# Elementwise chains kept in place in PSUM in a four-layer image network on one core

## The chip, the cores and the metric

The kernel runs on one core of a Trainium2 chip. The core has five engines that each work through their own queue of instructions in order and wait for each other by semaphores: TensorE (PE, matrix products into PSUM), VectorE (DVE), ScalarE (ACT), GpSimd (POOL) and SyncE (SP, which here only issues DMA transfers). SBUF is the large on-chip memory; PSUM is the small one that the matrix products write, in eight banks of 512 float32 columns by 128 partitions. The metric is the device time of one execution in microseconds; three runs of the kernel before gave 12745.85, 12742.49 and 12727.7, median 12742.49.

## The reference

Input and output are 8 images of 64 channels of 64x64, float32. Four layers follow each other.

- Layer 0: attention over the 4096 pixels with softmax(x^T x / 8) and values relu(bn(w1 x)), then a 3x3 depthwise convolution, batch norm and relu, a 1x1 convolution with batch norm, and the residual: `return out + x`.
- Layer 1: two blocks of window attention, 8x8 windows, 8 heads of 8 channels, each with an MLP. The second block shifts the image by four pixels, and windows at the wrap get a mask of -100 on the scores: `attn = softmax(q k^T + bias + mask)`.
- Layer 2: nine taps, each the shifted image times a factor by pixel and one by channel, summed; then a leaky relu, `a = where(out >= 0, out, 0.1 * out)`, a 1x9 convolution and a residual.
- Layer 3: a state-space scan in four directions with 128 channels and 16 states, h = h * exp(dt * A) + dt * B * u, y = sum(C * h); then `y = ln(y) * silu(z)`, a projection and a residual; then `gelu(aggr(...)) * x` added to the result, where aggr mixes four depthwise convolutions of different resolution.

## The kernel before, in words

Images go in pairs, p = 0 to 3, two images of 64 channels filling the 128 partitions. For each pair a generator `front(p)` does layers 0 to 2 and the inputs of the scan (`layer0`, `layer1`, `layer2`, `scan_sources`), `scans(p)` does the recurrence, and `back(p)` does what follows the scan. `scans` runs its own steps and, between them, pulls pieces of the generators beside it: `front(p+1)` and `back(p-1)`. So the front of pair 0 runs without scans, the scans of pairs 0, 1 and 2 run beside a front (and, from pair 1 on, a back), and the scans of pair 3 have only `back(2)` and, in their last steps, `back(3)` beside them. The numbers that the generators yield are costs; `scans` pulls until the sum of yields keeps pace with its steps. From the order so written a scheduler makes the order in each engine's queue when the program is built.

A scan step handles two of the 16 states over 512 pixels: POOL forms B * du for both (`products`, L1754, 128x1024), ACT forms exp(dt * A) into a PSUM bank (L1776), DVE runs the recurrence (L1779), POOL or DVE multiplies with C (L1790, L1793), and PE sums over the states (L1805). B and C rows come by DMA from rows that each unit wrote before (`fetch`, L1746, and `inputs`, L1729).

PSUM is given out by `bank`: three banks with the tag "f" serve front and back, three with the tag "da" the scans, one "acc" (through `total`) and one "y". While `turn` is not negative, in the first front and when only `back(3)` is left, `bank` alternates between "f" and "da".

The places that the change touches, all on tiles of 128x512 or 128x256 float32:

- `layer0`, last part: per chunk of 512 pixels nine DVE taps, ACT's relu (L1342), a matmul into the bank `pw` (L1344), ACT's batch norm from `pw` into the SBUF tile `t` (L1346), DVE's addition X + t (L1348).
- `window_row`, `scores`: two banks of scores from PE (L1431); DVE adds the bias and writes SBUF (L1444); where a window lies at the wrap DVE adds the mask in SBUF (L1448, 30 instructions per pair, all in the second block); ACT takes the exponential (L1449); PE multiplies with the values (L1459).
- `layer2`: PE sums nine taps into `acc` (L1576); ACT copies `acc` to the tile `t1` (L1580); DVE takes max(0.1 * acc, t1) into the padded tile `a` (L1581), which nine matmuls read (L1584). There are two tiles `a`, for even and odd chunks.
- `back`, first part: per chunk and image a matmul into the bank `pc` (L1235), the square on ACT (L1237), its mean by PE into `pv` (L1239), two ACT instructions to the inverse deviation `sd` (L1241, L1242); DVE forms u = pc * g * sd in SBUF (L1845) and u = (u + b) * z (L1846), and PE projects u (L1847) into `po`, which DVE adds to X (L1849).
- `back`, last part: nine DVE taps into `sacc` (L1251), a copy to SBUF by ACT (L1886), four matmuls into the bank `pa` (L1888, L1892), GELU by ACT from `pa` into the SBUF tile `ge` (L1900), DVE's product ge * F (L1901) and DVE's addition X + ge (L1902), and the store of the output.

Of the kernel before, what the change touches and what calls it, by code (L numbers as in the profile page):

```python
# [9 lines left out]
F32 = mybir.dt.float32  # L10
AF = mybir.ActivationFunctionType
ALU = mybir.AluOpType
# [5 lines left out]
P = 128  # L18
CH = 512
# [1140 lines left out]
class _Direct:  # L1160
# [104 lines left out]
    def layer0(self, p):  # L1265


        nc, tc, w, net, half = self.nc, self.tc, self.w, self.net, self.HALF
        X = self.flat("X")
        nc.sync.dma_start(X, self.net.x[2 * p : 2 * p + 2].rearrange("b c h w -> (b c) (h w)"))  # L1270
        att = self.padded("att")
        VT = self.flat("VT").rearrange("p (t c) -> p t c", c=P)

        def at(rows, t):
            return X[rows, t * P : (t + 1) * P]

        with self.work("w0") as wk:
            for g in range(8):
                pv = self.bank("pval", (P, 4, P))
                nc.tensor.matmul(pv, lhsT=net.ones[0:1, :], rhs=net.b1row.rearrange("o a c -> o (a c)").unsqueeze(1).to_broadcast([1, 4, P]), start=True, stop=False)  # L1280
                for j in range(4):
                    nc.tensor.matmul(pv[:, j, :], lhsT=at(slice(0, P), 4 * g + j), rhs=net.w1bd, start=False, stop=(j == 3))
                nc.scalar.activation(VT[:, 4 * g : 4 * g + 4, :], pv, AF.Relu)
                yield 3

            parts = wk.tile([P, 2, 32, NCH], F32, name="parts", tag="parts", bufs=1)
            self.dense = 1
            for jc in range(NCH):
                po = self.total("po")

                def weigh(t, es):
                    for im in range(2):
                        nc.tensor.matmul(  # L1293
                            po[half[im]], lhsT=VT[:, t, half[im]], rhs=es[im], start=(t == 0), stop=(t == 31)
                        )

                last = None
                for t in range(32):
                    ss = [self.bank(f"s{im}") for im in range(2)]
                    for im in range(2):  # L1300
                        nc.tensor.matmul(  # L1301
                            ss[im], lhsT=at(half[im], t), rhs=X[half[im], jc * CH : (jc + 1) * CH], start=True, stop=True
                        )
                    es = []
                    for im in range(2):
                        e = wk.tile([P, CH], F32, name="e", tag="e", bufs=6)
                        nc.scalar.activation(  # L1307
                            e, ss[im], AF.Exp, scale=C**-0.5, accum_out=parts[:, im, t, jc : jc + 1]
                        )
                        es.append(e)  # L1310
                    if last is not None:
                        weigh(*last)
                    last = (t, es)
                    yield 3.6
                weigh(*last)
                nc.vector.tensor_copy(self.rows(att, jc), self.img(po))  # L1316

            self.dense = 0
            sums = net.sums[:, p]
            nc.vector.tensor_reduce(sums, parts, AX.X, ALU.add)  # L1320
            rec = wk.tile([P, 2, 32], F32, name="rec", tag="rec", bufs=1)
            nc.vector.reciprocal(rec, sums)
            for g in range(8):
                pr = self.bank("prec")
                for j in range(4):
                    for im in range(2):
                        nc.tensor.matmul(
                            pr[half[im], j * P : (j + 1) * P],
                            lhsT=rec[:, im, 4 * g + j : 4 * g + j + 1].to_broadcast([P, 64]),
                            rhs=w["ident"],  # L1330
                            start=True,
                            stop=True,
                        )
                d = self.rows(att, g)
                nc.vector.tensor_tensor(d, d, self.img(pr), ALU.mult)
                yield 3
        with self.work("w0b") as wk:
            for c in range(NCH):
                acc = self.bank("cacc", (P, 8, 64))
                yield from self.dwconv(acc, att, 8 * c, 8, w["dw2"], None, 0.52)  # L1340
                cv = wk.tile([P, 8, 64], F32, name="cv", tag="cv")
                nc.scalar.activation(cv, acc, AF.Relu, scale=net.bn23[:, 0:1], bias=net.bn23[:, 1:2])  # L1342
                pw = self.bank("pw")
                nc.tensor.matmul(pw, lhsT=w["w3bd"], rhs=cv, start=True, stop=True)  # L1344
                t = wk.tile([P, CH], F32, name="t", tag="t")
                nc.scalar.activation(t, pw, AF.Identity, scale=net.bn23[:, 2:3], bias=net.bn23[:, 3:4])  # L1346
                x = X[:, c * CH : (c + 1) * CH]
                nc.vector.tensor_tensor(x, x, t, ALU.add)  # L1348
                yield 2.25
        return X  # L1350

# [64 lines left out]
    def window_row(self, i, wy, X, now, ahead, wk):  # L1416
# [6 lines left out]
        def scores(x):  # L1423

            es = []
            ss = [self.bank(f"w_s{g}", (P, 2, 4, 64)) for g in range(2)]
            for j in range(2):
                for g in range(2):
                    for im in range(2):
                        rows = slice(64 * im + 32 * g, 64 * im + 32 * g + 32)  # L1430
                        nc.tensor.matmul(  # L1431
                            ss[g][half[im], j],
                            lhsT=K[rows, 64 * (x + j) : 64 * (x + j) + 64],
                            rhs=qx[rows, x + j],
                            start=True,
                            stop=True,
                        )
            kinds = [2 * (wy == 7) + (x + j == 7) if shift else 0 for j in range(2)]
            for g in range(2):
                hs = slice(4 * g, 4 * g + 4)  # L1440
                e = self.share(self.wide, 4 + self.nth % 4).rearrange("p (j h q) -> p j h q", j=2, h=4)
                self.nth += 1
                b = bias[:, 0, hs].unsqueeze(1).to_broadcast([P, 2, 4, 64])
                nc.vector.tensor_tensor(e, ss[g], b, ALU.add)  # L1444
                for j in range(2):
                    if kinds[j]:
                        m = net.smask[:, kinds[j] : kinds[j] + 1].to_broadcast([P, 4, 64])
                        nc.vector.tensor_tensor(e[:, j], e[:, j], m, ALU.add)  # L1448
                nc.scalar.activation(e, e, AF.Exp)  # L1449
                es.append(e)  # L1450
            return es
# [83 lines left out]
    def layer2(self, X):  # L1535
# [11 lines left out]
        with tc.tile_pool(name="w2", bufs=2) as wk:  # L1547
            net.load(wk, (5,))
            cf = net.channel_filters(X, wk, self.pf, "f")
            for c in range(NCH):  # L1550
# [25 lines left out]
                    nc.tensor.matmul(acc, lhsT=w["ident"], rhs=tap, start=(t == 0), stop=(t == TAPS - 1))  # L1576
                    yield 2.7
                a = acts[c % 2]
                t1 = wk.tile([P, 8, 64], F32, name="t1", tag="t1", bufs=1)
                nc.scalar.activation(t1, acc, AF.Copy)  # L1580
                nc.vector.scalar_tensor_tensor(a[:, :, 4:68], acc, 0.1, t1, ALU.mult, ALU.max)  # L1581
                py = self.total("py", (P, 8, 64))
                for t in range(TAPS):
                    nc.tensor.matmul(  # L1584
# [242 lines left out]
    def back(self, p):  # L1827
# [5 lines left out]
        with tc.tile_pool(name="w4", bufs=2) as wk:  # L1833
            for c in reversed(range(NCH)):
# [3 lines left out]
                for im in range(2):  # L1838
                    y = self.share(big, im)
                    z = self.share(big, 2 + im)  # L1840
                    nc.sync.dma_start(y, self.kept["y", 2 * p + im][:, cols])
                    nc.sync.dma_start(z, self.kept[2 * p + im][2][:, cols])
                    pc, sd = self.normed(wk, lambda pc: [(pc, y)], w["cen128"], w["avg128"], net.eps[:, 0:1])
                    u = wk.tile([P, CH], F32, name="u", tag="u")
                    nc.vector.scalar_tensor_tensor(u, pc, w["on_g"], sd, ALU.mult, ALU.mult)  # L1845
                    nc.vector.scalar_tensor_tensor(u, u, w["on_b"], z, ALU.add, ALU.mult)  # L1846
                    nc.tensor.matmul(po[half[im]], lhsT=w["opT"], rhs=u, start=True, stop=True)  # L1847
                    yield 4.2
                nc.vector.scalar_tensor_tensor(X[:, cols], po, w["outproj_b"], X[:, cols], ALU.add, ALU.add)  # L1849
# [5 lines left out]
        with tc.tile_pool(name="w5", bufs=1) as wk:  # L1855
# [25 lines left out]
            for c in range(NCH):  # L1881
# [7 lines left out]
                for i in range(1, 4):  # L1889
# [6 lines left out]
                        start=False,  # L1896
                        stop=(i == 3),
                    )
                ge = wk.tile([P, 8, 64], F32, name="ge", tag="ge", bufs=2)
                last = nc.scalar.activation(ge, pa, AF.Gelu, bias=w["aggr_b"])  # L1900
                nc.vector.tensor_tensor(ge, ge, self.rows(F, c), ALU.mult)  # L1901
                nc.vector.tensor_tensor(X[:, cols], X[:, cols], ge.rearrange("p a b -> p (a b)"), ALU.add)  # L1902
                nc.sync.dma_start(out[:, cols], X[:, cols])
                yield 3.5
            net.log_exp(last)
# [51 lines left out]
```

## Time and profile before

| what | value |
|---|---|
| median of the runs (lowest, highest) | 12742.49 us (12727.7, 12745.85) |
| the profiled execution | 12767.64 us |
| its span, first to last instruction | 12765.8 us |
| mean granted clock of TensorE | 0.819 |
| front of pair 0, no scans | about 0 to 1830 us |
| layer 0's residual in the fronts of pairs 1, 2, 3 (L1348) | 2832 to 2957, 5876 to 5998, 8832 to 8955 us |
| shifted window attention of pairs 1, 2, 3 (L1444) | 3420 to 3745, 6451 to 6764, 9411 to 9721 us |
| back's first part of pairs 0, 1, 2, 3 (L1845) | 4514 to 4797, 7473 to 7763, 10431 to 10988, 12413 to 12662 us |
| back's last part of pairs 0, 1, 2, 3 (L1901) | 4849 to 4965, 7823 to 7938, 11209 to 11542, 12708 to 12757 us |

The profile gives for each engine its busy time, and for groups of equal instructions the busy time, the mean duration and the idle time of the engine just before them with what ended it. An engine's busy time includes time in which an instruction has started and is held up inside the engine; a wait for a semaphore, before it starts, counts as idle. So a group whose instructions do equal work and differ in duration tells of a hold-up inside. The stages of the table run one after the other, and each has an engine of its own that is fullest; the share of an engine over the whole span says little of any of them.

### The profile page before, as it was taken

The page shows a single profiled execution, that of the slowest core. Times are in us where ns is not written, and L with a number is a line of the kernel's source. Part 1 is how long each engine was busy: PE and PEld are TensorE (multiplying, and loading weights), DVE is VectorE, ACT ScalarE, POOL GpSimd, SP SyncE. Part 2 cuts the span into 40 slices and gives each one's busy share as a digit, 9 for nine tenths or more (in the row PEclk, how much of TensorE's full clock was granted, in tenths as well). Part 3 has the DMA queues.
Part 4 walks back from the last instruction along what each step waited for, and adds up shares of the span by engine and source line. Part 5 has one row for each costly group of instructions (what it writes and reads, how often), then busy time and mean ns, then how long its engine had stood idle before and what let it go on. Part 6 is the DMA issues. An engine that isn't in the chain of part 4 may idle for free. (4 is left out here: it accounts for less than half of the span.)

```text
span 12765.8 us, 142485 instructions
## 1 busy us (share of the span) xinstructions
PE 9843.7 (77%) x46358; PEld 3333.1 (26%) x46358; DVE 8687.9 (68%) x10259; ACT 7009.2 (55%) x15693; POOL 7550.7 (59%) x3844
## 2 busy tenths in 40 slices
PE   9888879987887667997888756997888855555556
PEld 2255222223342112222443211222433211111111
DVE  0122256777786776668776679467777679998878
ACT  5533247765663655665665555665566365455444
POOL 0000026677776683667776676467777567777874
PEclk9966779997888778998888877998888967777667
DMA  0000024544443462444443454344444356556554
GB/s 19 1 1 1 6 98 145 150 146 133 133 128 111 145 189 81 138 140 145 125 131 113 128 176 144 93 140 142 126 134 129 100 174 183 170 165 186 171 172 123
DMA packets 779703, 1575.84 MB, mean 123 GB/s; under 512 B 89280, under 2 KB 89408, under 8 KB 778176
## 3 DMA queue, kind: packets, MB, share of 16 engines
q1 hardware_dynamic: 754752, 1510.30, 39.4%
q10 hardware_dynamic: 24192, 56.32, 1.2%
q8 instruction: 367, 6.01, 0.2%
q14 instruction: 392, 3.21, 0.1%
HBM read 1197.16 MB, written 100.66 MB: 102 GB/s over the span
## 5 line engine op out<-in xcount | busy, mean ns | idle before, releaser
L1754 POOL TENSOR_TENSOR vd<-B,du 128x1024 f32<-128x1024 f32 x2048 | 4821.4, 2371 | 3295.1 <-DMA B<-rows 2016.1
L1805 PE MATMUL yd<-vd,pack 128*64 128x512 f32 x8192 | 2946.2, 738 | 933.7 <-POOL vd L1793 595.3
L1776 ACT ACTIVATE dad<-du,As 128x512 f32<-128x512 f32 x4096 | 2733.8, 682 | 1122.5 <-DVE vd L1793 458.5
L1779 DVE TENSOR_TENSOR_SCAN hd<-dad,carry,vd 128x512 f32<-128x512 f32 x1992 | 2497.0, 1267 | 480.0 <-ACT dad L1776 324.4
L1793 POOL TENSOR_TENSOR vd<-hd,C 128x512 f32<-128x512 f32 x1290 | 1659.8, 1290 | 1046.7 <-DVE hd L1779 1030.0
L1779 DVE TENSOR_TENSOR_SCAN dad<-dad,carry,vd 128x512 f32<-128x512 f32 x1592 | 2004.8, 1273 | 166.6 <-ACT dad L1776 164.4
L1790 POOL TENSOR_TENSOR vd<-hd,C 128x1024 f32<-128x1024 f32 x491 | 1158.1, 2359 | 735.5 <-DVE hd L1779 406.6
L1307 ACT ACTIVATE e<-s 128x512 f32<-128x512 f32 x2048 | 1200.2, 591 | 628.3 <-PE s L1301 626.5
L1301 PE MATMUL s<-X 64*128 64x512 f32 x4096 | 1435.8, 646 | 79.6 <-ACT e L1307 58.8
L1805 PEld LDWEIGHTS yd<-vd,pack 128*64 128x64 f32 x8192 | 667.0, 160 | 2815.0 <-issue 1214.6
L1793 DVE TENSOR_TENSOR vd<-dad,C 128x512 f32<-128x512 f32 x1824 | 1207.5, 673 | 239.6 <-ACT carry L1787 232.0
L1293 PE MATMUL po<-e,VT 128*64 128x512 f32 x4096 | 1207.8, 623 | 16.9 <-ACT e L1307 10.2
L1459 PEld LDWEIGHTS w_av<-vals,wide 64*64 64x64 f32 x16384 | 678.1, 173 | 209.7 <-ACT wide L1449 106.3
L1459 PE MATMUL w_av<-vals,wide 64*64 64x9 f32 x16384 | 705.6, 224 | 34.8 <-ACT wide L1449 34.6
L1787 ACT ACTIVATE carry<-hd 128x1 f32<-128x1 f32 (+1 forms) x1559 | 307.6, 200 | 697.1 <-DVE hd L1779 681.0
L1301 PEld LDWEIGHTS s<-X 64*128 64x128 f32 x4096 | 393.4, 186 | 1107.5 <-issue 832.6
L1787 ACT ACTIVATE carry<-dad 128x1 f32<-128x1 f32 x1594 | 268.1, 168 | 698.3 <-DVE dad L1779 688.9
L1717 PE MATMUL pdd<-xs,xdt 128*128 128x512 f32 x512 | 375.7, 824 | 334.6 <-issue 103.1
L1444 DVE TENSOR_TENSOR wide<-w_s,bias 128x512 f32<-128x512 f32 x512 | 327.7, 680 | 254.5 <-PE w_s L1431 246.5
L1449 ACT ACTIVATE wide<-wide 128x512 f32<-128x512 f32 x512 | 309.5, 626 | 318.7 <-DVE wide L1444 194.3
L1239 PE MATMUL pv<-n_sq,pack 128*128 128x512 f32 x576 | 364.5, 718 | 144.0 <-ACT n_sq L1237 130.0
L1316 DVE COPY att<-po 128x512 f32<-128x512 f32 x32 | 21.7, 679 | 643.3 <-PE po L1293 643.3
(246 smaller groups left out, 11137.5 us busy)
## 6 DMA issues: line engine op xcount, KB each, us to landing
B<-rows SPq DMA_DIRECT2D x2048, 256.0 KB, 3.6
C<-rows SPq DMA_DIRECT2D x2048, 256.0 KB, 3.5
du<-du SPq DMA_DIRECT2D x512, 512.0 KB, 5.9
xs<-xt SPq DMA_DIRECT2D x128, 256.0 KB, 3.6
xs<-xc SPq DMA_DIRECT2D x128, 256.0 KB, 3.8
xc<-xcv ACTq DMA_DIRECT2D x64, 256.0 KB, 2.1
zs<-z ACTq DMA_DIRECT2D x64, 256.0 KB, 3.8
xt<-XT ACTq DMA_DIRECT2D x32, 512.0 KB, 4.6
```

Source lines behind the costliest of these rows:

```text
L1293: nc.tensor.matmul(po[half[im]], lhsT=VT[:, t, half[im]], rhs=es[im], start=(t == 0), stop=(t == 31))
L1301: nc.tensor.matmul(ss[im], lhsT=at(half[im], t), rhs=X[half[im], jc * CH : (jc + 1) * CH], start=True, stop=True)
L1307: nc.scalar.activation(e, ss[im], AF.Exp, scale=C**-0.5, accum_out=parts[:, im, t, jc : jc + 1])
L1459: nc.tensor.matmul(self.av[half[im], x % 4 + j, h, :], lhsT=es[h // 4][half[im], j, h % 4, :], rhs=V[half[im], x + j, h, :], start=True, s ...
L1717: nc.tensor.matmul(pd, lhsT=net.xdt[:, k, :], rhs=x, start=True, stop=True)
L1754: self.nc.gpsimd.tensor_tensor(v, self.twice(st["B"]), self.units[i // 8]["du"][:, :, 1], ALU.mult)
L1776: nc.scalar.activation(da, u["du"][:, j, 0], AF.Exp, scale=net.As[:, k, n : n + 1])
L1779: nc.vector.tensor_tensor_scan(along(to), along(da), along(v[:, j]), first, ALU.mult, ALU.add)
L1787: nc.scalar.activation(cs, ends, AF.Copy)
L1790: st["w"] = nc.gpsimd.tensor_tensor(v, h, self.twice(CC), ALU.mult)
L1793: m = engine.tensor_tensor(v[:, j], hs[j], CC, ALU.mult)
L1805: m = nc.tensor.matmul(u["y"][self.HALF[j]], lhsT=w["fold"], rhs=st["v"][:, j], start=(i % 8 == 0), stop=(i % 8 == 7))
```

## The change

Five chains of elementwise instructions change the place of an intermediate. In `layer0` ACT writes the batch norm back into the bank `pw`, and DVE adds from there. In `scores` DVE adds the masks to the scores in their bank first, and the bias addition, which writes SBUF, comes after. In `layer2` ACT copies `acc` into the padded tile `a`, and DVE takes the maximum there in place; the tile `t1` goes. In `back` the first product writes `pc` in its bank, and the second reads it from there; GELU, and the product with F, stay in the bank `pa`, and X is added from there. The SBUF tiles `t`, `t1` and `ge` are gone. No instruction of the computation is added or removed. Each bank is given back after its last reader, which is now a later instruction: DVE's addition at `pw` and `pa`, the second product at `pc`, the bias addition after the masks at the scores.

```diff
@@ -1342,10 +1342,9 @@
                 nc.scalar.activation(cv, acc, AF.Relu, scale=net.bn23[:, 0:1], bias=net.bn23[:, 1:2])
                 pw = self.bank("pw")
                 nc.tensor.matmul(pw, lhsT=w["w3bd"], rhs=cv, start=True, stop=True)
-                t = wk.tile([P, CH], F32, name="t", tag="t")
-                nc.scalar.activation(t, pw, AF.Identity, scale=net.bn23[:, 2:3], bias=net.bn23[:, 3:4])
+                nc.scalar.activation(pw, pw, AF.Identity, scale=net.bn23[:, 2:3], bias=net.bn23[:, 3:4])
                 x = X[:, c * CH : (c + 1) * CH]
-                nc.vector.tensor_tensor(x, x, t, ALU.add)
+                nc.vector.tensor_tensor(x, x, pw, ALU.add)
                 yield 2.25
         return X
 
@@ -1441,11 +1440,11 @@
                 e = self.share(self.wide, 4 + self.nth % 4).rearrange("p (j h q) -> p j h q", j=2, h=4)
                 self.nth += 1
                 b = bias[:, 0, hs].unsqueeze(1).to_broadcast([P, 2, 4, 64])
-                nc.vector.tensor_tensor(e, ss[g], b, ALU.add)
                 for j in range(2):
                     if kinds[j]:
                         m = net.smask[:, kinds[j] : kinds[j] + 1].to_broadcast([P, 4, 64])
-                        nc.vector.tensor_tensor(e[:, j], e[:, j], m, ALU.add)
+                        nc.vector.tensor_tensor(ss[g][:, j], ss[g][:, j], m, ALU.add)
+                nc.vector.tensor_tensor(e, ss[g], b, ALU.add)
                 nc.scalar.activation(e, e, AF.Exp)
                 es.append(e)
             return es
@@ -1576,9 +1575,8 @@
                     nc.tensor.matmul(acc, lhsT=w["ident"], rhs=tap, start=(t == 0), stop=(t == TAPS - 1))
                     yield 2.7
                 a = acts[c % 2]
-                t1 = wk.tile([P, 8, 64], F32, name="t1", tag="t1", bufs=1)
-                nc.scalar.activation(t1, acc, AF.Copy)
-                nc.vector.scalar_tensor_tensor(a[:, :, 4:68], acc, 0.1, t1, ALU.mult, ALU.max)
+                nc.scalar.activation(a[:, :, 4:68], acc, AF.Copy)
+                nc.vector.scalar_tensor_tensor(a[:, :, 4:68], acc, 0.1, a[:, :, 4:68], ALU.mult, ALU.max)
                 py = self.total("py", (P, 8, 64))
                 for t in range(TAPS):
                     nc.tensor.matmul(
@@ -1842,8 +1840,8 @@
                     nc.sync.dma_start(z, self.kept[2 * p + im][2][:, cols])
                     pc, sd = self.normed(wk, lambda pc: [(pc, y)], w["cen128"], w["avg128"], net.eps[:, 0:1])
                     u = wk.tile([P, CH], F32, name="u", tag="u")
-                    nc.vector.scalar_tensor_tensor(u, pc, w["on_g"], sd, ALU.mult, ALU.mult)
-                    nc.vector.scalar_tensor_tensor(u, u, w["on_b"], z, ALU.add, ALU.mult)
+                    nc.vector.scalar_tensor_tensor(pc, pc, w["on_g"], sd, ALU.mult, ALU.mult)
+                    nc.vector.scalar_tensor_tensor(u, pc, w["on_b"], z, ALU.add, ALU.mult)
                     nc.tensor.matmul(po[half[im]], lhsT=w["opT"], rhs=u, start=True, stop=True)
                     yield 4.2
                 nc.vector.scalar_tensor_tensor(X[:, cols], po, w["outproj_b"], X[:, cols], ALU.add, ALU.add)
@@ -1896,10 +1894,9 @@
                         start=False,
                         stop=(i == 3),
                     )
-                ge = wk.tile([P, 8, 64], F32, name="ge", tag="ge", bufs=2)
-                last = nc.scalar.activation(ge, pa, AF.Gelu, bias=w["aggr_b"])
-                nc.vector.tensor_tensor(ge, ge, self.rows(F, c), ALU.mult)
-                nc.vector.tensor_tensor(X[:, cols], X[:, cols], ge.rearrange("p a b -> p (a b)"), ALU.add)
+                last = nc.scalar.activation(pa, pa, AF.Gelu, bias=w["aggr_b"])
+                nc.vector.tensor_tensor(pa, pa, self.rows(F, c), ALU.mult)
+                nc.vector.tensor_tensor(X[:, cols], X[:, cols], pa.rearrange("p a b -> p (a b)"), ALU.add)
                 nc.sync.dma_start(out[:, cols], X[:, cols])
                 yield 3.5
             net.log_exp(last)
```

## The prediction

> **What bounds the kernel now.** I read the page first, then the groups of VectorE (DVE) instructions by line, then the timeline of DVE and GpSimd (POOL) around one slow instruction, then busy time by stage, the waits of TensorE (PE) and POOL in those stages, and last the chain at the end.
>
> ```profile
> span 12765.8 us, 142485 instructions
> PE 9843.7 (77%) x46358; PEld 3333.1 (26%) x46358; DVE 8687.9 (68%) x10259; ACT 7009.2 (55%) x15693; POOL 7550.7 (59%) x3844
> ```
>
> No engine is full over the whole span, so each stage must be asked. The groups of the edited DVE lines, with L1849 for comparison (busy us, mean ns of one, idle before):
>
> ```profile
> L1846 DVE SCALAR_TENSOR_TENSOR u<-u,pack,big 128x512 f32<-128x512 f32 x64 | 112.5, 1758 | 0.2
> L1448 DVE TENSOR_TENSOR wide<-wide,smask 128x256 f32<-128x256 f32 x120 | 99.1, 871 | 0.5
> L1901 DVE TENSOR_TENSOR ge<-ge,F 128x512 f32<-128x512 f32 x32 | 40.2, 1257 | 3.7 <-ACT ge L1900 3.7
> L1348 DVE TENSOR_TENSOR X<-X,t 128x512 f32<-128x512 f32 x32 | 39.4, 1230 | 4.5 <-ACT t L1346 4.5
> L1902 DVE TENSOR_TENSOR X<-X,ge 128x512 f32<-128x512 f32 x32 | 36.7, 1146 | 0.2
> L1849 DVE SCALAR_TENSOR_TENSOR X<-po,pack,X 128x512 f32<-128x512 f32 x32 | 23.8, 745 | 29.2 <-PE po L1847 27.4 <-PE yd L1805 1.7
> ```
>
> L1846 and L1849 do the same operation on the same shape in the same stage, yet one takes 1758 ns and the other 745. L1846 reads two tensors from SBUF (u, z); L1849 reads one from PSUM (po) and one from SBUF. The other four slow groups also read two SBUF tensors. Their shortest members are 722, 407, 671, 676 and 677 ns, their longest 12752, 2607, 2773, 2770 and 2727. Sorted by whether a POOL instruction is running when they start, L1846 averages 1948 ns (54 of them) with POOL and 735 (10) without; L1448 1850 (38) and 417 (82). L1849 averages 743 (24) and 751 (8). The timeline, first DVE and then POOL:
>
> ```profile
> 3564.05 3.92 DVE L1448 TENSOR_TENSOR wide<-wide,smask 128x256 f32<-128x256 f32 x2
> 3567.89 0.68 DVE L1793 TENSOR_TENSOR vd<-dad,C 128x512 f32<-128x512 f32 x1
> ...
> 3563.92 2.36 POOL L1790 TENSOR_TENSOR vd<-hd,C 128x1024 f32<-128x1024 f32 x1
> 3566.23 1.46 POOL L1793 TENSOR_TENSOR vd<-hd,C 128x512 f32<-128x512 f32 x1
> ```
>
> Two masks that need 0.8 us together take 3.92: the first ends when POOL's instruction ends, and the second waits again. Every later DVE instruction (scans, products) is queued behind. By stage (us; busy of PE, PEld, DVE, ACT, POOL; granted clock, DMA share, GB/s):
>
> ```profile
> 2830.00:2960.00 130.00, 66.62 (x137) 16.24 (x136) 125.15 (x142) 58.38 (x122) 109.71 (x53) 0.67 0.48 142
> 3420.00:3745.00 325.00, 291.27 (x3082) 156.75 (x3082) 249.99 (x325) 175.42 (x356) 227.57 (x111) 0.81 0.40 120
> 4514.00:4797.00 283.00, 192.06 (x402) 43.59 (x398) 229.26 (x222) 151.39 (x324) 263.08 (x127) 0.77 0.60 185
> 4849.00:4965.00 116.00, 63.40 (x133) 22.11 (x134) 114.58 (x135) 62.56 (x98) 57.31 (x31) 0.78 0.41 123
> 10431.00:10990.00 559.00, 327.96 (x731) 71.14 (x728) 498.49 (x513) 291.26 (x662) 461.52 (x244) 0.74 0.60 185
> ```
>
> They are: layer 0's depthwise convolution with the residual (DVE full), the shifted attention with its masks (PE 90%), back's normalisation (POOL 93%), back's GELU part (DVE full), and back's normalisation beside the last pair's scans (DVE 89%). From the chain at the end:
>
> ```profile
> 12437.36 2.85 DVE u L1846
> 12472.15 2.15 DVE u L1846
> ```
>
> [...] the longest of 1824 DVE products at L1793 (PSUM and SBUF) is 693 ns, 1297 of them started while POOL ran. [...] L1444 (PSUM source) 680 ns against 677 for L1902 undisturbed. [...]
>
> **The change part by part.** Times are of the profiled execution, 12767.64 us, 1.8 us around its span; it is 25 us above the median of 12742.49, so I subtract the sum from the median. The DVE, POOL, PE and SP instruction counts stay; ACT gets one more table load. The scheduler shifts some neighbours among the scans; I price that at 0, at most 10 either way.
>
> Afterwards L1846, L1901, L1902, L1348 and L1448 read PSUM and at most one SBUF tensor, so the block should vanish. The excess in DVE time, busy of the stage less the undisturbed cost:
> - Masks: 30 per pair of images cost 11.72 in the front that has no scans beside it, and 31.01, 28.08, 28.29 in the other three: excess 19.3+16.4+16.6 = 52.3. The new form is nearest to L1475 (PSUM source, 128x256, 417 ns), no dearer.
> - L1846: 16 per pair at 727 ns are 11.6; measured 28.86, 25.18, 35.07, 23.43: excess 17.3+13.6+23.5+11.8 = 66.2.
> - L1348: 5.50 quiet; 12.83, 9.79, 10.57 beside scans: 16.7.
> - L1901: 5.49 quiet; 9.19, 15.34, 9.96: 18.0. L1902: 5.47 quiet; 12.37, 9.79, 9.03: 14.8.
>
> That is 168 us of DVE time, the most that is directly there. What of it lies on the path:
> - Layer 0's residual, DVE 125.2 of 130: next in line is the following convolution, on DVE itself. 0.9 of 16.7 = 15.
> - GELU part for the first two pairs, DVE 114.6 of 116: excess (3.7+6.9)+(9.9+4.3) = 24.8, taken at 0.9 = 22.
> - Masks: PE sets the pace. Its wait for the exponentials (w_av for L1449) is 5.2, 8.9 and 8.9 in the three masked stretches and 0.2, 0, 0 in the unmasked ones: 22.8. Its wait for DVE's w_h is 46.1 against 28.4: 17.7 more. So between 23 and 41; I take 30.
> - L1846 for the first two pairs (excess 30.9): POOL is the fullest, 263 of 283, and idles mostly for a B row from DMA (16.5 and 15.3), not for DVE. But POOL is blocked in its turn: its instructions that overlap an edited one are together 5.7 and 5.9 us over their median. I take 12; all 31 if DVE decides.
> - The third pair's back, beside the last scans: excess 23.5+4.5+3.6 = 31.6 with DVE at 89-90%; POOL waits 63.9 for B rows, which come at the end of a chain through all engines. I take 0.65 = 20.
> - The last pair's back at the end: eight pieces of L1846 on the chain are 14.9 us, 5.8 undisturbed. Of the 9 I take 7, as other work stands close behind.
>
> Gain 106. Costs: the first mask now precedes the bias addition, so a score bank is freed up to 0.42 us later per mask: rows 0-6 have one masked step (7 x 0.42), the last row four with two masks (8 x 0.42), 6 us per pair, 19 at most over the three pairs where three banks serve the front; I take 3, since the second bias addition also no longer stands behind a blocked mask. pc is held for one to two more DVE instructions, pw and pa until DVE's addition ends: nothing, because PE's next matmul of the chain (po at L1847, pw at L1344, pa at L1888) waits for ACT or DVE work that ends no earlier; if that cover were absent, 64 x 2.0 (the second instruction and a scan between) + 32 x 1.5 + 32 x 2.5 = 256. The table load is 1.28. [...] Layer 2's copy goes into a tile whose last reader finished a chunk earlier; ACT already idles 268.5 for acc (L1580), and L1581 still reads one PSUM and one SBUF tensor: 0, within 2.
>
> 106 - 3 - 1 = 102, so 12742 - 102 = 12640.
>
> **Rivals.**
> - *All of it is on the path* (each stage follows its DVE queue): 168 and POOL's own blocking of about 12 give 12562. For it: everything behind a blocked instruction waits. Against: PE at 90% and POOL at 93% in two stages. 0.15.
> - *Only the DVE-full stages pay*: 15+22+7, and half of the third pair, 10, less 4 = 50: 12692. For it: POOL and B rows. 0.2.
> - *Nothing to see*: freed DVE time is eaten by waits for B rows, which stay as long: 12725 to 12760. 0.05. Against: two stages have DVE over 95% busy.
> - *Slower, by held banks*: with three banks in the front's pool, pc, pw and pa kept through a DVE queue of scans stall PE's next matmul. Full price 256 + 19, less 106: 12912. It decides once more than 0.8 us of each of the 128 longer holds is waited for. Against: at L1344 PE waits for ACT (365.2), at L1888 for ACT (513.1); no wait for a bank stands out. 0.07.
> - *It doesn't do what it says*: the block remains with one PSUM input. L1849 and L1793 speak against it; part of the "nothing" chance.
>
> **How the numbers follow.** The forecast has 0.53, the two rivals on the same side 0.35, nothing 0.05, slower 0.07. The measurement can tell about 0.2% (25 us): faster means under 12717. Inside the forecast the stage shares may each be wrong by a third, 35 us, and the shifted neighbours by 10: 12595 to 12685. With the two rivals beside it the range is 12555 to 12712. Faster 0.88, same 0.05, slower 0.07.
>
> **What would show it.** L1846's successor near 735 ns with a longest below 0.8 us; masks near 417; the two GELU products and the residual near 680. PE's wait for the exponentials in the masked stretches near 1 instead of 8; the GELU part about 10 us shorter per pair; back's normalisation for the first two pairs only 5 to 8 shorter. Wrong if those groups stay above 1 us, if PE shows new waits for DVE at L1235, L1239 or L1344, or if waits of POOL for B rows grow by what DVE gained.

## The result and the profile after

The changed kernel takes 12647.43 us (median; 12642.81 to 12668.15), the kernel before 12744.17 in the same comparison: a ratio of 0.9921, 95% interval 0.9905 to 0.9936. That is 97 us less; 102 were predicted, 12640 against 12647. The profiled execution took 12668.15 us, near 100 us less than the one before.

The page of the kernel after, its span and the engines' busy time:

```profile
span 12666.3 us, 142495 instructions
PE 9810.4 (77%) x46358; PEld 3319.4 (26%) x46358; DVE 8518.4 (67%) x10259; ACT 7014.7 (55%) x15694; POOL 7504.2 (59%) x3844
```

DVE lost 169.5 us of busy time with the same number of instructions, POOL 46.5. The groups of the edited DVE lines after (busy us, mean ns of one, idle before and its releaser):

```profile
L1844 DVE SCALAR_TENSOR_TENSOR u<-pc,pack,big 128x512 f32<-128x512 f32 x64 | 47.0, 735 | 0.2
L1446 DVE TENSOR_TENSOR w_s<-w_s,smask 128x256 f32<-128x256 f32 x120 | 46.7, 423 | 58.6 <-PE w_s L1430 58.2
L1898 DVE TENSOR_TENSOR pa<-pa,F 128x512 f32<-128x512 f32 x32 | 22.1, 690 | 5.9 <-ACT pa L1897 5.9
L1347 DVE TENSOR_TENSOR X<-X,pw 128x512 f32<-128x512 f32 x32 | 21.6, 675 | 4.9 <-ACT pw L1345 4.9
L1899 DVE TENSOR_TENSOR X<-X,pa 128x512 f32<-128x512 f32 x32 | 21.7, 679 | 0.2
```

The means went from 1758, 871, 1257, 1230 and 1146 ns to the undisturbed ones, and the longest members from 12752, 2607, 2773, 2770 and 2727 to 752, 433, 742, 689 and 687 ns. The idle time at L1446 is no new loss: it is the wait for the scores that stood at the bias addition before, which now comes second (that one's idle time fell from 254.5 to 191.2 us). The timeline at a masked step of the first shifted attention beside scans, DVE and then POOL:

```profile
3545.79 0.76 DVE L1446 TENSOR_TENSOR w_s<-w_s,smask 128x256 f32<-128x256 f32 x2 [0.49 <-PE w_s L1430]
3546.46 1.28 DVE L1447 TENSOR_TENSOR wide<-w_s,bias 128x512 f32<-128x512 f32 x2
...
3544.04 2.37 POOL L1752 TENSOR_TENSOR vd<-B,du 128x1024 f32<-128x1024 f32 x1
3546.34 2.39 POOL L1788 TENSOR_TENSOR vd<-hd,C 128x1024 f32<-128x1024 f32 x1
3548.67 1.29 POOL L1791 TENSOR_TENSOR vd<-hd,C 128x512 f32<-128x512 f32 x1
```

Two masks and two bias additions pass in 2 us while POOL works; the two masks alone took 3.92 before. The stages again (us; busy of PE, PEld, DVE, ACT, POOL; granted clock, DMA share, GB/s), in the order of the prediction's windows:

```profile
2829.00:2949.00 120.00, 60.27 (x128) 14.55 (x124) 115.16 (x139) 56.22 (x119) 101.63 (x51) 0.70 0.49 148
3406.00:3727.00 321.00, 294.69 (x3146) 156.63 (x3146) 235.36 (x332) 178.42 (x362) 230.99 (x114) 0.81 0.41 125
4504.00:4783.00 279.00, 185.59 (x398) 42.66 (x394) 210.50 (x220) 150.37 (x321) 255.32 (x126) 0.80 0.61 187
4835.00:4947.00 112.00, 71.93 (x138) 23.26 (x138) 108.06 (x138) 64.75 (x99) 55.97 (x31) 0.74 0.45 134
10364.00:10908.00 544.00, 316.21 (x726) 68.64 (x722) 473.87 (x510) 290.37 (x662) 453.67 (x242) 0.75 0.62 189
```

In the third line DVE lost 18.8 us and the stage 4; POOL, the fullest engine, lost 7.8 with one instruction fewer in the window. In the fourth DVE lost 6.5 and the stage 4.

Where the time went is read by the lead of the kernel after at the same instruction in both profiles (start before less start after). Each stage is taken from the first to the last start of its edited DVE instructions (the bias additions for the attention). The last row is a stage without an edited instruction (residual additions, L1532):

| stage | predicted | growth of the lead |
|---|---|---|
| layer 0's residual, pairs 1, 2, 3 | 15 | 5 + 6 + 6 = 17 |
| shifted attention, pairs 1, 2, 3 | 30 - 3 | 4 + 5 + 12 = 21 |
| back's normalisation, first two pairs | 12 | 4 + 8 = 12 |
| GELU, first two pairs (first to last product) | 22 | 5 + 7 = 12 |
| back of the third pair, both parts | 20 | 12 + 2 between + 4 = 18 |
| back of the last pair | 7 | 14 |
| second MLP of pair 1's front | 0 | -9 |

The other 13 of the 98 us that stand at the last GELU product are steps of both signs in and between the other stages. They are not all small: 8 us are gained behind the first pair's last GELU product, and in pair 2's front 9 are gained between the residual and the first window attention and 11 lost in that attention. A single row is less sure than it looks, too: in the runs below that leave a stage as it was, its lead against this same profile still moves, by up to 13 us in one shifted attention, 12 in one first part of back and 8 in one GELU part.

### The profile page after: what moved, and what is told of

Read it like the earlier page. It is cut to its first block, busy times and chain, and to the rows that moved or that the text cites. A ratio compares the mean times of both kernels' runs of the same rounds, so it can differ in the third digit from the quotient of the medians.

```text
span 12666.3 us, 142495 instructions
## 1 busy us (share of the span) xinstructions
PE 9810.4 (77%) x46358; PEld 3319.4 (26%) x46358; DVE 8518.4 (67%) x10259; ACT 7014.7 (55%) x15694; POOL 7504.2 (59%) x3844
## 5 line engine op out<-in xcount | busy, mean ns | idle before, releaser
L1777 DVE TENSOR_TENSOR_SCAN dad<-dad,carry,vd 128x512 f32<-128x512 f32 x1592 | 2005.7, 1274 | 169.5 <-ACT dad L1774 165.4
L1575 PE MATMUL acc<-taps,pack 128*128 128x512 f32 x576 | 374.1, 782 | 107.6 <-DVE taps L1574 107.2
L1447 DVE TENSOR_TENSOR wide<-w_s,bias 128x512 f32<-128x512 f32 x512 | 328.4, 680 | 191.2 <-PE w_s L1430 187.1
```

Source lines behind the costliest of these rows:

```text
L1777: nc.vector.tensor_tensor_scan(along(to), along(da), along(v[:, j]), first, ALU.mult, ALU.add)
```

## Experiments

The theory: a DVE instruction with two SBUF inputs waits for POOL, as the times of L1846 suggest (1948 ns where it started while POOL ran, 735 where not), and one PSUM operand ends the wait, as those of L1849 do (743 and 751). The rivals: the longer hold of the banks costs or gains; the scheduler's slightly different order made the difference; what counts is DVE time, however it is spent.

**One part of the change at a time**, each on the kernel before. In the diffs of this section `...` stands for lines left out.

The masks alone:

```diff
-                nc.vector.tensor_tensor(e, ss[g], b, ALU.add)
...
-                        nc.vector.tensor_tensor(e[:, j], e[:, j], m, ALU.add)
+                        nc.vector.tensor_tensor(ss[g][:, j], ss[g][:, j], m, ALU.add)
+                nc.vector.tensor_tensor(e, ss[g], b, ALU.add)
```

> The kernel before with the masks alone added in the score banks. Blocking theory (DVE with two SBUF inputs waits for POOL): the masks fall from 871 to about 420 ns on average, 52 us of DVE time; PE sets the pace there, so 20 to 30 us of the span go, about 12720. If everything behind a blocked instruction were on the path: 52, 12692. If the longer hold of the score banks decides: PE waits more for DVE at the score matmuls, 0 to 19 us slower.

Measured: 0.9985 (0.9978 to 0.9991), 19 us less (11 to 28), the masks at 424 ns. Just below what was expected.

Back's first product alone:

```diff
-                    nc.vector.scalar_tensor_tensor(u, pc, w["on_g"], sd, ALU.mult, ALU.mult)
-                    nc.vector.scalar_tensor_tensor(u, u, w["on_b"], z, ALU.add, ALU.mult)
+                    nc.vector.scalar_tensor_tensor(pc, pc, w["on_g"], sd, ALU.mult, ALU.mult)
+                    nc.vector.scalar_tensor_tensor(u, pc, w["on_b"], z, ALU.add, ALU.mult)
```

> The kernel before with back's first product alone kept in pc. Blocking theory: the second product falls from 1758 to about 735 ns, 66 us of DVE time, of which about 34 us reach the span (12 in the two backs that POOL fills, 15 beside the last scans, 7 at the end), about 12710. All on the path: 66, 12678. Held banks: pc is kept 2 us longer 64 times, up to 128 us slower.

Measured: 0.9968 (0.9956 to 0.9981), 41 us less (24 to 56). The second product fell to 735 ns. In its profile the lead grows by 4, 5, 15 and 15 us in the four backs' first parts: 9 where 12 were expected, 15 where 15 were, and 15 at the end where 7 were.

GELU and its product alone:

```diff
-                last = nc.scalar.activation(ge, pa, AF.Gelu, bias=w["aggr_b"])
-                nc.vector.tensor_tensor(ge, ge, self.rows(F, c), ALU.mult)
+                last = nc.scalar.activation(pa, pa, AF.Gelu, bias=w["aggr_b"])
+                nc.vector.tensor_tensor(pa, pa, self.rows(F, c), ALU.mult)
...
```

> The kernel before with GELU and its product alone kept in pa. Blocking theory: both DVE instructions fall to about 680 ns, 33 us of DVE time, of which 27 reach the span because DVE is full there, about 12717. Held banks: pa is kept for two DVE instructions more 32 times, up to 80 us slower.

Measured: 0.9985 (0.9977 to 0.9992), 19 us less (10 to 29); both instructions at 692 and 681 ns. Less than the 27 expected, which lie inside the interval.

The residual alone:

```diff
-                nc.scalar.activation(t, pw, AF.Identity, scale=net.bn23[:, 2:3], bias=net.bn23[:, 3:4])
+                nc.scalar.activation(pw, pw, AF.Identity, scale=net.bn23[:, 2:3], bias=net.bn23[:, 3:4])
...
-                nc.vector.tensor_tensor(x, x, t, ALU.add)
+                nc.vector.tensor_tensor(x, x, pw, ALU.add)
```

> The kernel before with the first layer's residual alone added from pw. Blocking theory: 1230 to about 680 ns, 17 us of DVE time where DVE is full, 15 us of the span, about 12729. Held banks: up to 48 us slower. The four parts should add up to the change, 96 us, if they don't depend on each other.

Measured: 0.9995 (0.9987 to 1.0003), 6 us less, between 17 less and 4 more. The instruction fell to 677 ns, but the gain is not to be told from nothing; the 15 us expected lie just inside the interval.

Layer 2's copy alone:

```diff
-                nc.scalar.activation(t1, acc, AF.Copy)
-                nc.vector.scalar_tensor_tensor(a[:, :, 4:68], acc, 0.1, t1, ALU.mult, ALU.max)
+                nc.scalar.activation(a[:, :, 4:68], acc, AF.Copy)
+                nc.vector.scalar_tensor_tensor(a[:, :, 4:68], acc, 0.1, a[:, :, 4:68], ALU.mult, ALU.max)
```

> The kernel before with layer 2's copy alone put into the padded tile. Theory: both DVE forms read one PSUM and one SBUF tensor, nothing was blocked, 0 within 10 us. Rival, that the smaller number of SBUF tiles is worth something: faster by more than 10.

Measured: 0.9996 (0.9988 to 1.0005), not to be told from nothing. By their ratios the five parts add up to 90 us, and the whole is 101 here and 105 in a second comparison below: within the noise of five such differences, some 25 us, the parts add.

**Do the held banks count?** The operands of before, and after the instruction where the change gives each bank back a DVE copy of one column of it, so that it is held as long (128 added instructions, their output unused). The score banks of the masks are not in this run.

```diff
                     nc.vector.scalar_tensor_tensor(u, u, w["on_b"], z, ALU.add, ALU.mult)
+                    hd = wk.tile([P, 1], F32, name="hb", tag="hb")
+                    nc.vector.tensor_copy(hd, pc[:, 0:1])
...
```

> The kernel before, operands unchanged, with one DVE copy of one column of pc, pw and pa after the instruction that ends their use in the change, so that the banks are held as long as there (128 added instructions). Theory: the hold costs nothing, the small instructions some 0.1 us each of which part is on the path: 0 to 15 us slower, L1846 still near 1.8 us. Held-bank rival: 50 us slower or more, with PE waiting for DVE at the next pc, pw or pa. Rival that holding or ordering rather than operands made the gain: faster.

Measured: 0.9991 (0.9983 to 0.9999), 11 us less and not more. The added copies took 146 ns each. L1846's counterpart stays slow, so the operands, not the hold, make it so. The counterpart, and PE's waits for the copies:

```profile
L1848 DVE SCALAR_TENSOR_TENSOR u<-u,pack,big 128x512 f32<-128x512 f32 x64 | 106.1, 1658 | 0.0
PE pval L1280 <- DVE hb L1908: 2.3, 1, 2.3
```

This one, of 2.3 us, is all that PE's matmuls wait for a bank so held (weight loads wait for the copies five more times, 4.4 us in all). The hold of the banks at these three places is free, as predicted. The small gain was not expected, and it is in the direction that the rival of holding or ordering named; with 1 to 22 us it is far from the 97 of the change. In this profile the longest wait of L1846's counterpart is 4.57 us, where before it was 12.75; that would make 8 us, but the link was only seen, not tested.

**Blocked time against plain time.** One more DVE product with an unused output, after back's second product: once of two SBUF tiles, u and z, as in the diff; once of PSUM and SBUF, with pc in u's place.

```diff
                     nc.vector.scalar_tensor_tensor(u, u, w["on_b"], z, ALU.add, ALU.mult)
+                    sc = wk.tile([P, CH], F32, name="sc", tag="sc", bufs=1)
+                    nc.vector.tensor_tensor(sc, u, z, ALU.mult)
```

> The kernel before with an unused product of u and z (both SBUF) after back's second product, 64 more DVE instructions. Blocking theory: it too waits for POOL, 1.5 to 2 us on average, 100 to 120 us of DVE time, 50 to 90 of the span. If position or in-place writing were the cause of the slow L1846: about 0.7 us each like the next run.

> The same with pc (PSUM) and z as the inputs of the unused product. Blocking theory: 0.68 us each, 44 us of DVE time, 20 to 40 of the span, so 30 to 50 faster than the run with two SBUF inputs. Its bank pc is held as in the change. If operands don't matter: the same time as that run.

The added product in the first and in the second of these runs:

```profile
L1848 DVE TENSOR_TENSOR sc<-u,big 128x512 f32<-128x512 f32 x64 | 89.7, 1401 | 0.3
```

```profile
L1848 DVE TENSOR_TENSOR sc<-pc,big 128x512 f32<-128x512 f32 x64 | 43.4, 678 | 0.0
```

Same place, same number, same output, one operand different: 1401 against 678 ns, and 1.0025 (1.0017 to 1.0033) against 0.9993 (0.9984 to 1.0001), 41 us apart. The operand is the cause of the long duration here. The time of the kernel could also hang on the order, which the scheduler makes anew for each: at 704 of the 10323 places in DVE's order another line stands. Both sizes were missed. The first run was expected to be 50 to 90 us slower than before and is 32 slower (22 to 42); the second was expected to be 20 to 40 slower and is not slower at all. Either plain DVE time is free there, or it is paid and something else was won: the longest L1846 in this run is 4.56 us again, though one residual addition, L1348, took 10.9. To tell these apart, the same two products were added to the kernel after, where no product of back is blocked; the diff has pc and z, the other run u and z:

```diff
                     nc.vector.scalar_tensor_tensor(u, pc, w["on_b"], z, ALU.add, ALU.mult)
+                    sc = wk.tile([P, CH], F32, name="sc", tag="sc", bufs=1)
+                    nc.vector.tensor_tensor(sc, pc, z, ALU.mult)
```

> The change, with the unused product of pc (PSUM) and z after back's second product. Nothing else in back is blocked here, so this prices plain DVE time. If DVE time on its own pays at the shares of the prediction (about half): 44 us more of DVE time, 15 to 25 us above the change, about 12660. If the run with the same product on the kernel before showed the rule, that only blocked time pays: within 8 of the change, about 12640.

> The change, with the unused product of u and z, both in SBUF. It is the only blocked product of back's first part: about 1.8 us each, 115 us of DVE time. Blocking theory: 30 to 55 us above the run with one SBUF input, 12690 to 12710, which is what the change won at this place. If operands don't matter: the same as that run.

```profile
L1846 DVE TENSOR_TENSOR sc<-pc,big 128x512 f32<-128x512 f32 x64 | 43.7, 683 | 0.0
```

```profile
L1846 DVE TENSOR_TENSOR sc<-u,big 128x512 f32<-128x512 f32 x64 | 99.5, 1554 | 0.3
```

Measured: 0.9914 (0.9901 to 0.9927) with one SBUF input, against 0.9918 (0.9904 to 0.9932) for the change itself in the run below: 43.7 us of plain DVE time cost nothing that can be seen, and by the two intervals less than about 20 us. With two SBUF inputs 0.9948 (0.9935 to 0.9962): 56 us more of DVE time cost 43 us (19 to 67), as much as the change won at this place. That the same exchange costs 41 us in one kernel and 43 in the other, with different orders, speaks against the order as the cause. In the first back's window of the run with one SBUF input DVE is busy 225 of 279 us, against 210.5 of 279 in the change, and in the third 491 of 550 against 474 of 544: plain work, whose output nothing waits for, mostly filled gaps here. The blocked time did not: its 56 us more cost 43. Part of why is seen: the wait is mutual, and POOL's products, summed beyond 30 ns over the median of their kind, are 33 us too long with the blocked product and 17 without it. That a scheduler which knows an instruction's length but not its wait sets the rest around it is an argument, not a result.

**The change again, and one step further.** Back's two smaller depthwise convolutions add to an SBUF tile from an SBUF tile. Their sums were put into a PSUM bank:

```diff
-                    cv = wk.tile([P, n, n], F32, name=f"cv{i}", tag=f"cv{i}")
+                    cv = self.bank(f"cv{i}", (P, n, n))
```

> The change itself again, as the comparison for the next run: about 0.992 of the kernel before, 12640 to 12655.

> The change, and besides the depthwise convolutions of back's two smaller pooled images (16x16 and 8x8, 64 DVE instructions with two SBUF inputs that still average 673 and 464 ns against 478 and 277 undisturbed) summed in a PSUM bank instead of SBUF. Blocking theory: they fall to about 480 and 280 ns, 14 us of DVE time where DVE is full, about 10 us of the span, 12635. If the gains of the change came from the scheduler's order alone: no difference, within 10 either way.

Measured: the change 0.9918 (0.9904 to 0.9932), 12637.99 us; the step further 0.9911 (0.9898 to 0.9924), 12630.66. The DVE instructions of these convolutions in the change and then in the step further (both sizes together):

```profile
L436 DVE SCALAR_TENSOR_TENSOR cv<-pool,pack,cv 128x256 f32<-128x256 f32 (+1 forms) x64 | 36.4, 568 | 0.0
L434 DVE TENSOR_SCALAR cv<-pool,pack 128x256 f32<-128x256 f32 (+1 forms) x8 | 6.4, 801 | 0.0
```

```profile
L436 DVE SCALAR_TENSOR_TENSOR cv<-pool,pack,cv 128x256 f32<-128x256 f32 (+1 forms) x64 | 24.2, 378 | 0.0
L434 DVE TENSOR_SCALAR cv<-pool,pack 128x256 f32<-128x256 f32 (+1 forms) x8 | 3.5, 441 | 0.0
```

The 64 taps with two SBUF inputs fell from 673 and 464 to 477 and 279 ns by size, with nothing longer than 0.49 us. The first tap of each, L434, fell too, although it has only one SBUF input (see the last section). The 7 us between the medians are of the size expected but inside the intervals, so it is not shown to beat the change; it beats the kernel before.

## Why the prediction was right

- **Which instructions are slow, and why.** What the prediction read from L1846 against L1849 and L1793 held for every edited line: the means of 871 to 1758 ns fell to 423 to 735. The runs with one operand exchanged show it at a single place, 1401 against 678 ns and 1554 against 683.
- **The 168 us of DVE time.** DVE's busy time fell by 169.5.
- **Masks, 30 less 3.** Right mechanism, sized too high: 21 in the stages, 19 alone. The prediction expected PE's wait for the exponentials near 1 us per stretch; it fell from 5.2, 8.9 and 8.9 to 0, 4.4 and 4.4. Its wait for w_h fell from 46.1 to 39.3. It was taken for granted that these waits would go nearly wholly, and other waits rose, among them one for POOL's products: in the three stretches together PE waits 99.4 us before and 84.8 after, 15 less; in the other runs it is 93 to 100 where the masks are left alone and 78 to 83 where they are edited. The other 6 us of the 21 are PE's own busy time, 849 before and 842 after, which lies between 830 and 847 in the runs that leave the masks alone; they are not shown to be the masks'.
- **L1846 beside a full POOL, 12.** Met: 12 in the change, 9 alone. POOL's own lengthening, the measure that the prediction chose, fits this: POOL's excess beyond 30 ns over the medians fell from 59 to 14 us over the span. Since the lead of these two stages moves by several us in runs that don't edit them, the size is not shown more closely.
- **GELU, 22 and the third pair's share.** 12 in the two stretches, 19 for the part alone against about 27. A share of 0.9 for a stage with DVE at 99% was too high; after the change DVE is at 108 of 112 us.
- **The third pair, 20.** 18. Its waits for B rows stayed, 63.9 before and 65.5 after, as the argument for the smaller share had it.
- **The end, 7.** Mis-sized: 14, and 15 for the part alone. More than the whole excess there (11.8) was won; that other work stands close behind, for which the prediction took a part off, is not seen.
- **Held banks, 0.** Right for `pc`, `pw` and `pa`, by the hold run, and the one table load more, 1.28 us, and the PSUM operands cost nothing that shows: the edited DVE instructions took 735, 423, 690, 675 and 679 ns, in the order of the groups above, against 735, 417, 683, 686 and 682 for those of before that started while no POOL instruction ran, and ACT's two in-place instructions even fell from 771 to 745 and from 687 to 662 ns.
- **Neighbours shifted by the scheduler, 0 within 10.** Pair 1's second MLP gave back 9 us, and 11 in the second profile of the change. No edited instruction lies in it, but the loss comes with the masks' edit: in the masks alone and in the five runs that contain the change, this stretch (first to last L1532 or its counterpart) takes 93 to 96 us at a granted clock of 0.84 to 0.91; in the kernel before and the seven other runs 84 to 87 us at 0.92 to 0.97. In it PE is busy 62.5 us before and 69.4 after. Why the clock is lower there stays open, and so does how much of the loss it makes.

The mechanism was right; that the sum came so close was in part luck. Stage by stage the predicted terms make 103 us and the measured ones 85: -6 for the masks, -10 for GELU, -9 in the MLP, -2 for the third pair, against +7 at the end and +2 for the residual. The 13 us of steps that the prediction had no term for made up most of the difference.

## What to carry to other kernels

Look for DVE groups of one shape whose longest member is far above its shortest, and sort them by whether GpSimd was running: where both inputs are in SBUF, a result that already stands in PSUM may be better left there (97 us here), and the longer hold of the bank is worth a test rather than a fear (at three places here, PE's matmuls waited 2.3 us for it). The excess is hidden time inside busy time; plain DVE work in the same place may be free while time spent blocked is not (43.7 us that cost nothing to be seen, and 56 more that cost 43). Price it stage by stage, by what the fullest engine of that stage waits for.

## What the runs showed of the hardware that was not expected

A blocked DVE instruction didn't always get its turn at the end of the POOL instruction it met. Before, one L1846 took 12.75 us while seven POOL instructions ended, as these views of DVE and then POOL show, and in four of the five single-part runs the longest was again 12.75 us (the fifth has no blocked L1846). Of the other 37 of that group that took over 1.2 us, 33 saw one POOL instruction end.

```profile
10536.31 12.75 DVE L1846 SCALAR_TENSOR_TENSOR u<-u,pack,big 128x512 f32<-128x512 f32 x1
...
10532.23 9.25 POOL L1754 TENSOR_TENSOR vd<-B,du 128x1024 f32<-128x1024 f32 x4
10541.44 1.26 POOL L1793 TENSOR_TENSOR vd<-hd,C 128x512 f32<-128x512 f32 x1
10542.66 2.34 POOL L1754 TENSOR_TENSOR vd<-B,du 128x1024 f32<-128x1024 f32 x1
10544.95 1.26 POOL L1793 TENSOR_TENSOR vd<-hd,C 128x512 f32<-128x512 f32 x1
10546.17 2.34 POOL L1754 TENSOR_TENSOR vd<-B,du 128x1024 f32<-128x1024 f32 x1
```

One SBUF input was enough in two cases. The first tap of the two small convolutions (L434, TENSOR_SCALAR with one tensor input) was started while POOL ran once for each size in the profile of the change, and took 2329 and 1946 ns; the other six took 404 to 407 and 304 to 310. With the result in PSUM it took 548 and 347 while POOL ran, and 534 to 543 and 336 to 342 otherwise: longer alone, but not held up. What sets this form apart was not tested.

POOL paid as well, but less (46.5 us of busy time went with the change, against 169.5 of DVE's): its product of 128x512, 1269 ns as a rule, took 1.46 us next to the blocked masks. The longest of these products, 3.31 us before and 3.36 after, met a DVE instruction that the change doesn't touch (L1862 before, L1860 after).
